# A planner's due times set anew, scores that wait for their evicted projections, and products of ones during the first loads

## The chip, the cores and the metric

The kernel runs on one core of one Trainium2 chip. The metric is the device time of one execution in microseconds (us). Each kernel is executed several times; the median and the spread are given, and one execution more is recorded by the hardware profiler. All arithmetic is in fp32.

The core's engines, as the profile names them: PE multiplies matrices (PEld is its loading of weights), DVE is the vector engine, ACT the scalar engine, POOL a second, slower vector engine, and SP issues DMA transfers. Each engine works off its own list of instructions in order. They wait for each other by semaphores. Products land in PSUM, in banks of 512 fp32 values for each of 128 partitions, and an engine has to evict them from there.

## The reference

Eight images of 64 x 64 pixels with 256 channels pass through two layers.

```python
# layer 0
q, k = split(x @ w_qkv + b_qkv);  v = k
ctx_h = sdpa(windows of 8 rows,    channels   0..127, 4 heads of 32)
ctx_v = sdpa(windows of 8 columns, channels 128..255, 4 heads of 32)
hv = hard_swish(v)
context = hard_swish(concat(ctx_h, ctx_v) + depthwise_conv3x3(hv) + dw_bias)
x = context @ w_out + b_out
# layer 1: attention over all 4096 pixels, with one head of 32
f, g, h = x @ kf + bf, x @ kg + bg, x @ kh + bh
beta = softmax(g @ f.T)
out = gamma * ((beta @ h) @ kv + bv) + x
```

kf, kg, kh and kv are the weights divided by their spectral norm, which the kernel works out at the start. sdpa is softmax attention, with a scale of 1/sqrt(32). A window has 512 pixels.

## The kernel before

**Units and steps.** The work of an image is cut into units: eight horizontal windows h0 to h7, eight vertical windows v0 to v7, and two halves l0 and l1 of the global attention, each with 2048 queries against all keys. A unit of h has 4 steps, one of v 3, one of l 32. All eight images run as one list of steps. The h0 of the next image is placed between v7 and l0 of this one, so that PE has scores to work on while f, g and h are being made.

A step does the same on PE everywhere: the products of the scores s (L849 and L825 in the windows, L1064 in l), from which ACT makes the weights p by two instructions of exp (L606), and then the products of the step before with the values, num (L878, L871, L1080). In v two of three steps have three passes instead of two (L825, with exps L838 and L843). The weights lie in a ring of eight slots. Before a slot is written again, DVE must have added up what it holds (L887, L895, L902; in l L1095) or a DMA issued by POOL must have (L1104, L1106), since the sums over the keys are needed for the softmax: DVE and DMA add steps together, and a product with ones on PE adds over the partitions (sum_h and sum_v L917, sum_l L1117). A v unit uses all eight slots.

**Fillers.** Between scores and values PE does everything else: the projections pq of an image (L326; tile m = 0 is q and m = 2 is k of the channels of h, called near; m = 1 and 3 are q and k of the channels of v, called far), the sums, the products pf (L987) and phd (L1014) that make f, g and h with w_out folded into their weights (wcomb), the transposes ph of h (L1028), and the results (w_out and the part of layer 1, evicted to ot_l at L1146). A projection has 16 products in four pieces. All fillers share one bank of PSUM, named mm, so one of them can only begin once the one before it has been evicted. The results take the banks of the scores instead. A result has two pieces, one for each 128 output channels, which take PE 8 us each.

**Around it.** x comes in tiles of 512 pixels (L663) into a pool of two buffers. Each q and k is evicted by ACT with its bias (qh L682, kh L697, qv L685). DVE transposes k (kt L766), and it goes through DRAM (kvia L771) and comes back as values (vs L782). The contexts of v go through DRAM as well (via_v L940, shuf_v L945). The convolution's nine taps for a pair of windows are one ACT instruction (L752) and eight on DVE (L756). f and g go through a tile fg and are spread by ten issues for each piece (L1004, L1005). All of these transfers, loads and stores alike, are issued on one queue, SP, strictly in order.

**The planner.** The order of instructions isn't written out. A class Flow plays the program forward at build time. It keeps a clock for each engine, advanced by constants (SCORES 0.96, VALUES 0.88, PROD 0.86, DRAIN 0.11 and so on, L71 to L77), and lanes of waiting tasks, each with a due step. The due steps come from the dictionary DUE (L49), as offsets from the first step of the unit that uses the task's outcome. `step` (L251) issues the scores, then urgent fillers, then the values, and then fills PE, ACT and DVE up to the clock. `require` issues whatever a step can't do without, no matter when it was due, and returns the time at which it ends. Before its scores a unit requires what stands in `u.ahead` (`unit_scores`, L1560): near q and near k for h, all far projections for v, and pf, ph and their transposes for l. The time that `require` returns for these is not used, so the planner's clock of PE goes on as if the scores could start at once. Near projections get their due steps at L1380 to L1386; for the first image first_near is added to both. The sum of an l unit is added at L1280, at a price of 1.5 products. Results wait in a lane of their own, and `apart` is the least number of steps between two pieces of them.

Of the kernel before, what the change touches and what calls it, by code (L numbers as in the profile page):

```python
# [17 lines left out]
P = 128  # L18
# [22 lines left out]
def side(h):  # L41
# [5 lines left out]
SLOTS = 8  # L47

DUE = dict(  # L49
    ahead1=104, ahead2=7, ahead3=1, ahead4=17, k0=-13, k1=52, k2=-18, k3=0, k4=-3, k5=18, k6=-3, k7=7,  # L50
    q0=70, q1=31, q2=-14, q3=-2, q4=70, q5=4, q6=0, q7=99, join_h0=38, join_h1=17, join_h2=23,
    join_h3=23, join_h4=-12, join_h5=26, join_h6=-17, join_h7=58, join_v0=26, join_v1=19, join_v2=20,
    join_v3=-25, join_v4=-148, join_v5=-22, join_v6=22, join_v7=-5, swish1=98, swish2=-48, swish3=-133,
    swish4=17, far_swish0=101, far_swish1=5, far_swish2=-23, far_swish3=28, far_swish4=46,
    far_swish5=-127, far_swish6=3, far_swish7=-2, result0=121, result1=-27, release_v=-9, norm_v=11,
    sums_v=-54, context_v=-34, clip_v=70, other=-91, first_ready=42, first_near=-1, first_k=1,
    first_q=-2, first_swish_v=-3, first_swish_h=54, first_conv_h=6, first_conv_v=22, near_k=-4,
    near_q=91, near_values=-10, clip=141, swish=12, conv_h0=168, conv_h1=16, conv_h2=24, conv_h3=39,
    conv_v0=17, conv_v1=23, conv_v2=29, conv_v3=69, tap=-21, join_h=-73, join_hl=24, join_v=1,
    context=-43, norm=18, release=-7, sums=66, add=26, adds_h=1, adds_v=0, group_h=0, group_v=1,  # L60
    add2=-44, add3=93, apart=6, fg0=-7, fg2=31, fg3=120, h0=32, h1=12, values_v=-74, near0=-55,
    spread0=4, spread1=72, spread_mid=61, conv_first=309, far_swish=-2,
)
INSIDE = 4
AHEAD = 16
# [4 lines left out]
SCORES, VALUES, PROD, TURN, DRAIN, PASS, THIRD = 0.96, 0.88, 0.86, 0.65, 0.11, 0.43, 0.5  # L70
EXP, EVICT, COPY, VIEW = 0.97, 0.62, 0.52, 0.42  # L71
# [26 lines left out]
class Flow:  # L98
# [5 lines left out]
    def __init__(self):  # L104
        self.t = 0
        self.clock = dict(pe=0.0, act=0.0, dve=0.0, sp=0.0)
        self.lanes = dict(pe=[], turn=[], act=[], dve=[], sp=[], pool=[], rows=[], res=[])
        self.open = None
        self.held, self.held_more, self.values_due = None, 0.0, False
        self.bank_free = 0.0  # L110
        self.half_end = self.exp_end = 0.0
        self.weights_free = self.mid_free = 0.0
        self.third = False
        self.apart = 0
        self.dve_last = None

    def add(self, lane, *args, **kw):
        task = Task(*args, **kw)
        task.lane = lane
        self.lanes[lane].append(task)  # L120
        return task
# [129 lines left out]
    def step(self, scores, values, passes=2, third=False):  # L251

        c = self.clock
        more = (passes - 2) * PASS
        rest = None
        self.third = passes > 2
        self.apart += 1
        self.values_due = True  # L260
        for task in self.waiting("res"):
            if self.apart >= DUE["apart"] and task.begin() <= c["pe"] + DRAIN or not scores:
                self.apart = 0
                c["pe"] = max(c["pe"] + DRAIN, self.half_end + LAG)
                while not task.done:
                    self.fill_act(c["pe"] + 4 * PROD)
                    self.run(task)
                    self.fill_dve()
        if scores:
            rest = scores()  # L270
            c["pe"] = max(c["pe"], self.banks()) + DRAIN + SCORES + more
            self.third = third
            self.half_end = max(c["act"], c["pe"] - more + PE_LAG, self.weights_free) + EXP
            if more:
                self.half_end = max(self.half_end, c["pe"] + PE_LAG) + EXP
            before, self.exp_end = self.exp_end, self.half_end + EXP
            c["act"] = self.exp_end
        else:
            before = self.exp_end
            c["pe"] = self.half_end = self.exp_end = max(c["pe"], c["act"], c["dve"]) + 3.0  # L280
        for task in sorted(self.waiting("turn"), key=lambda k: k.due):
            if self.begin(task) <= c["pe"] + 0.1:
                self.run(task)
        urgent = sorted((k for k in self.lanes["pe"] if k.due <= self.t), key=lambda k: k.due)
        if len(urgent) > 1 and urgent[0] in self.waiting("pe"):
            if self.begin(urgent[0]) <= c["pe"] + 0.1:
                self.require(urgent[0])
        if self.held:
            ready = self.held()
            c["pe"] = max(c["pe"] + DRAIN, before + LAG, ready + LAG) + VALUES + self.held_more  # L290
        self.held, self.held_more, self.values_due = values, more, False
        if rest:
            rest()
            if self.mid_free > self.exp_end - EXP:
                self.exp_end = c["act"] = self.mid_free + EXP
        self.fill_act(self.late(c["pe"]) - EVICT)
        self.fill_pe()
        self.fill_act(self.late(c["pe"]) + SLACK)
        self.fill_dve()
        for task in self.waiting("sp"):  # L300
            if task.begin() <= self.clock["pe"] + 0.5:
                self.run(task)

        for task in self.waiting("rows"):
            if task.begin() <= self.clock["pe"] + 0.5:
                self.run(task)
        for task in self.waiting("pool"):
            if task.begin() + BEHIND <= self.clock["pe"]:
                self.run(task)
        self.t += 1  # L310
# [19 lines left out]
def tile_attention_blocks(  # L330
# [18 lines left out]
    nc = tc.nc  # L349
# [14 lines left out]
    def mm_tile(name):  # L364
        return ps_mm.tile([P, TB], F32, tag="mm", name=name)
# [4 lines left out]
    ones = const.tile([P, P], F32, name="ones")  # L370
    nc.gpsimd.memset(ones, 1.0)
    three = const.tile([P, 1], F32, name="three")
    nc.gpsimd.memset(three, 3.0)
    three_e = const.tile([P, 1], F32, name="three_e")

    wqkv_sb = const.tile([P, 2, 2 * C], F32, name="wqkv_sb")
    wq = w_qkv.rearrange("(k p) m -> p k m", p=P)
# [142 lines left out]
    def attention(images, load_x, out_rows, exact):  # L520
# [17 lines left out]
        act = [state.tile([P, 2, 2 * TB], F32, name=f"act{i}") for i in range(NB // 2)]  # L538
# [656 lines left out]
        flow = Flow()  # L1195
# [56 lines left out]
        for u in units:  # L1252
            if not u.kind:
                continue
            e = u.t + u.steps
            w = [weights_ready(u.t + c) for c in range(u.steps)]
            if u.kind == "l":
# [12 lines left out]
                for c in range(0 if exact else u.steps):  # L1270
# [6 lines left out]
                    readers[u.t + c].append(task)  # L1277
                    gathered.append(task)
                total = flow.add(
                    "pe", [(u.sums, [("pe", PROD * (1 if exact else 1.5)), ("act", COPY)])], e + 1,  # L1280
                    [chain, *gathered[-2:]], ready=e, bank=True,
                )
                in_turn("sum", total)
# [1 line left out]
            else:  # L1285
# [12 lines left out]
                last = len(u.terms) - 1  # L1298
# [65 lines left out]
        for n, im in enumerate(ims):  # L1364
            last = ims[n - 1] if n else None
# [3 lines left out]
            for i in range(NB):  # L1369
                u = h[i]  # L1370
# [4 lines left out]
                start = last.l[0].t if last else 0  # L1375
# [4 lines left out]
                for m in (0, 2):  # L1380
                    near[i, m] = flow.add(
                        "pe", product_pieces(partial(im.project, i, m), 2, ("act", EVICT)),
                        (u.t + DUE["near_k" if m else "near_q"] + (0 if last else DUE["first_near"]))
                        if due is None else due, [], after, ready, True,
                    )
                early = start + inside_due(i, 0) if i in (1, 2) else u.t  # L1386
# [16 lines left out]
                for half in range(2):  # L1403
# [18 lines left out]
                    if p >= 0:  # L1422
# [3 lines left out]
                        if half and last and k == 0:  # L1426
                            due = min(due, start + inside_due(2 * HV[1], 0) + DUE["conv_first"])
                        tap = flow.add(
                            "act", [(partial(im.conv, p, half, (0,)), [("act", EXP)])],
                            due + DUE["tap"],  # L1430
                            scaled + [edges[q, half] for q in range(k, min(NB, k + 3)) if (q, half) in edges],
                            last.results[k] if last else [],
                        )
# [13 lines left out]
            context = {}  # L1447
# [74 lines left out]
        for n, im in enumerate(ims):  # L1522
            for i in range(INSIDE + 1 if n else 0, NB):
                more = [] if n else [im.far[i, 1], im.far[i, 3]]
# [31 lines left out]
        def left_by(kept):  # L1556

            return [k for n, mid in kept for k in ([last_mids[n]] if mid else readers[n])]

        def unit_scores(u, c):  # L1560
            if u.kind:
                flow.require(*u.ahead.get(c, ()))
                flow.weights_free = flow.require(*left_by(old[u.t + c][0]))
                if exact and c == 0 and flow.open:
                    flow.require(flow.open)
            rest = u.scores(c)
            if not rest:
                return None

            def then():  # L1570
                flow.mid_free = flow.require(*left_by(old[u.t + c][1]))
                rest()

            return then
# [8 lines left out]
        with tc.manual_schedule():  # L1583
            last = None
            steps = [(u, c) for u in units for c in range(u.steps)]
            passes = [3 if u.kind in ("h", "v") and c in u.passes else 2 for u, c in steps] + [2]
            for n, (u, c) in enumerate(steps):
                if c == 0 and n:
                    last = steps[n - 1][0]
# [31 lines left out]
        exact=False,  # L1621
# [4 lines left out]
    with tc.If(fine < 2 * P):  # L1626
        with tc.For_i(0, B) as b:
# [6 lines left out]
                exact=True,  # L1634
# [46 lines left out]
```

## Time and profile before

| | |
|---|---|
| time, median of 3 executions | 3267.01 us (3264.59 to 3268.1) |
| profiled execution, its own time | 3267.18 us |
| span of that execution in the trace | 3265.4 us |
| granted TensorE clock, mean | 0.999 |
| exps L606: busy, mean of one | 1612.8 us, 1024 ns |
| adds of l on DVE, L1095: busy, mean of one | 842.8 us, 1756 ns |
| convolution taps on DVE, L756: busy, mean of one | 654.0 us, 1278 ns |
| load of x (512 KB), issue to landing | 4.0 us |

The span begins with the first and ends with the last instruction, 1.8 us less than the time that is measured from outside. In the profile a line such as "s<-gq,f 32*128 32x512" reads: tile s is made from gq and f, with the partitions and elements of both operands. An arrow behind it names what the engine waited for. "Busy" of PE means that a product was in the array's pipeline. An image takes some 402 us. Image 4, which is looked at most, has its h7 at about 1760 us, its v0 to v7 from there to about 1865, and the l units behind that.

### The profile page before, as it was taken

Reading aid. Unit: us, or ns where it says so; the run is one execution under the profiler, and the core shown is the slowest. Engines: PE = TensorE matmul, PEld = TensorE weight load, DVE = VectorE, ACT = ScalarE, POOL = GpSimd, SP = SyncE. Lnnn points to the kernel's source line nnn. Section 1 sums busy time; section 2 is a strip of 40 time slices with the busy share of each in tenths; the row PEclk is TensorE's granted clock in tenths of the full one; section 3 lists DMA queues with packets and bytes.
Section 4 is the critical chain, followed back from the end, with each engine's and each line's share of the span. In section 5 each row is a group of like instructions: output and inputs, shape, how many; then the busy total and the mean of one; then the engine's idle time right before and its main releaser. Section 6 shows DMA issues by size and latency. Waiting matters only on the chain.

```text
span 3265.4 us, 83524 instructions
## 1 busy us (share of the span) xinstructions
PE 3218.2 (99%) x35348; PEld 1166.6 (36%) x35348; DVE 2659.7 (81%) x2426; ACT 2653.4 (81%) x3230; POOL 516.4 (16%) x786
## 2 busy tenths in 40 slices
PE   8999999999999999999999999999999999999998
PEld 3353233532335323343333433334323343234422
DVE  6898599975999669996699966998769986689865
ACT  6788788887888878888778887788877888778875
POOL 1002220022200222002210032100321003210132
PEclk9999999999999999999999999999999999999999
DMA  2235552356423564235642366423654236532465
GB/s 81 63 94 117 131 114 83 90 118 132 105 88 94 115 139 105 79 99 116 137 103 77 104 122 132 102 75 103 128 127 103 74 105 132 118 104 63 112 125 108
DMA packets 320655, 344.41 MB, mean 105 GB/s; under 512 B 33600, under 2 KB 198352, under 8 KB 320272
## 3 DMA queue, kind: packets, MB, share of 16 engines
q0 software_dynamic: 72000, 134.40, 23.2%
q1 hardware_dynamic: 246752, 204.04, 21.0%
q8 instruction: 280, 4.59, 0.6%
q14 instruction: 103, 0.84, 0.1%
q10 hardware_dynamic: 1520, 0.54, 0.1%
HBM read 99.78 MB, written 83.89 MB: 56 GB/s over the span
## 4 chain that ended last, share of the span: by engine, by line
PE 84%; DVE 9%; ACT 3%; DMA 2%; issue 1%; SPq 0%; DVEq 0%; ACTq 0%
PE s L1064 17%; PE num_l L1080 15%; PE pq L326 12%; PE s L849 8%; PE s L326 7%; PE num_h L878 6%; PE s L825 4%; PE num_v L871 4%; PE sum_v L917 3%; DVE act L756 3%; PE sum_h L917 3%; PE pf L987 1%; DVE acc_v L887 1%; PE num_v L878 1%; ACT p L606 1%
## 5 line engine op out<-in xcount | busy, mean ns | idle before, releaser
L606 ACT ACTIVATE p<-s 128x1024 f32<-128x1024 f32 x1664 | 1612.8, 1024 | 232.9 <-PE s L1064 143.8
L1095 DVE TENSOR_TENSOR acc_l<-acc_l,p 128x1536 f32<-128x1536 f32 x480 | 842.8, 1756 | 361.6 <-ACT p L606 357.4
L756 DVE SCALAR_TENSOR_TENSOR act<-hv,dw_sb,act 128x1024 f32<-128x1024 f32 x512 | 654.0, 1278 | 25.9 <-ACT act L752 16.5
L1064 PE MATMUL s<-gq,f 32*128 32x512 f32 x4096 | 594.1, 640 | 1.1 <-ACT ot_l L1146 1.1
L326 PE MATMUL pq<-x,wqkv_sb 128*32 128x256 f32 x8192 | 547.1, 381 | 14.0 <-DMA x<-in_xT 10.6
L1080 PE MATMUL num_l<-p,h_sb 128*32 128x512 f32 x4096 | 545.5, 605 | 0.3 <-ACT nums_l L1110 0.3
L326 PEld LDWEIGHTS pq<-x,wqkv_sb 128*32 128x32 f32 x8192 | 264.4, 110 | 431.8 <-issue 283.2
L849 PE MATMUL s<-qh,kh 32*128 32x512 f32 x2048 | 295.3, 640 | 14.0 <-ACT qh L682 13.9
L1106 POOL DMA_DIRECT2D acc_l<-p x240 | 210.3, 876 | 515.2 <-ACT p L606 477.7
L1106 POOL DMA_DIRECT2D row_l<-p x240 | 210.8, 878 | 426.9 <-ACT p L606 414.1
L878 PE MATMUL num_h<-p,vs 128*32 128x512 f32 x2048 | 272.0, 603 | 0.2 <-ACT nums_h L929 0.2
L1064 PEld LDWEIGHTS s<-gq,f 32*128 32x128 f32 x4096 | 168.7, 182 | 260.7 <-issue 247.1
L326 PE MATMUL s<-act,wout_sb 128*32 128x512 f32 x2048 | 229.2, 597 | 0.0
L1080 PEld LDWEIGHTS num_l<-p,h_sb 128*32 128x32 f32 x4096 | 80.7, 108 | 383.8 <-issue 371.3
L825 PE MATMUL s<-qv,kv 32*128 32x256 f32 x3072 | 214.3, 394 | 1.1 <-ACT p L843 0.8
L1146 ACT ACTIVATE ot_l<-s,bias_o 128x512 f32<-128x512 f32 x120 | 76.2, 684 | 161.3 <-PE s L326 154.5
L871 PE MATMUL num_v<-p,vs 128*32 128x256 f32 x3072 | 192.2, 383 | 0.0
L825 PEld LDWEIGHTS s<-qv,kv 32*128 32x128 f32 x3072 | 141.3, 183 | 80.5 <-issue 49.5
L1104 POOL DMA_DIRECT2D acc_l<-p x16 | 9.1, 566 | 1015.9 <-ACT sum_sb_h L626 508.8
L838 ACT ACTIVATE p<-s 128x1024 f32<-128x1024 f32 x128 | 131.8, 1030 | 33.5 <-PE s L825 33.4
L895 DVE TENSOR_TENSOR acc_h<-acc_h,p 128x2048 f32<-128x2048 f32 x64 | 146.1, 2282 | 7.8 <-ACT p L606 7.1
L887 DVE TENSOR_TENSOR acc_v<-p 128x2048 f32<-128x2048 f32 x64 | 146.3, 2286 | 6.4 <-PE sum_h L917 3.5
(153 smaller groups left out, 3211.5 us busy)
## 6 DMA issues: line engine op xcount, KB each, us to landing
acc_l<-p POOLq DMA_DIRECT2D x256, 256.0 KB, 3.3
row_l<-p POOLq DMA_DIRECT2D x256, 256.0 KB, 3.3
x<-in_xT SPq DMA_DIRECT2D x92, 512.0 KB, 4.0
kvia<-kt SPq DMA_DIRECT2D x128, 256.0 KB, 2.5
vs<-kvia SPq DMA_DIRECT2D x512, 64.0 KB, 2.1
out<-ot_l SPq DMA_DIRECT2D x120, 256.0 KB, 2.1
via_v<-nums_v SPq DMA_DIRECT2D x64, 256.0 KB, 2.1
shuf_v<-via_v SPq DMA_DIRECT2D x256, 64.0 KB, 2.1
```

The lines of the kernel that those rows point to most:

```text
L326: nc.tensor.matmul(out[quad(r), :], lhsT=lhsT[:, quad(r)], rhs=rhs, start=start, stop=stop)
L606: nc.scalar.activation(pt[:, 2 * z : 2 * z + 2, :], sc[z], AF.Exp, scale=scale)
L756: nc.vector.scalar_tensor_tensor(o, src, wt, o, ALU.mult, ALU.add)
L825: mm = nc.tensor.matmul(place_of(n, r, h, sc), lhsT=k[quad(r), t * P : (t + 1) * P], rhs=q[quad(r), side(h)], start=True, stop=True,)
L849: nc.tensor.matmul(row_of(sc, r), lhsT=k[quad(r), c * P : (c + 1) * P], rhs=q[quad(r), :], start=True, stop=not exact,)
L871: nc.tensor.matmul(u["num"][quad(r), side(h)], lhsT=vs[kind, i][:, r, t, :], rhs=place_of(n, r, h, (pt[:, :2], u["mid", c], pt[:, 2:])), s ...
L878: nc.tensor.matmul(u["num"][quad(r), :], lhsT=vs[kind, i][:, r, c, :], rhs=u[c][:, r, :], start=(c == 0), stop=(c == 3),)
L917: nc.tensor.matmul(u["sum"][quad(r), cols], lhsT=ones[:, :D], rhs=pt, start=(n == 0), stop=(n == last),)
L1064: nc.tensor.matmul(row_of(sc, r), lhsT=f4[quad(r), c * P : (c + 1) * P], rhs=gq[quad(r), z, :], start=True, stop=not exact,)
L1080: nc.tensor.matmul(u["num"][quad(r), :], lhsT=h_sb[:, c, :], rhs=u[c][:, r, :], start=(c == 0), stop=(c == 4 * NB - 1),)
L1095: nc.vector.tensor_add(acc, u[0][:, :rows, :] if c == 1 else acc, u[c][:, :rows, :])
L1106: nc.gpsimd.dma_start(out=u["row", c % 2], in_=u[c][:, rows, :], accum_op=ALU.add)
```

## The change

It has five parts. All values of DUE are set anew, and one key is new (first_near_q). `unit_scores` keeps the time at which the required tasks end, and `step` starts PE's clock for the scores no earlier than that. The sums of l are priced at two products instead of 1.5. Nine products of a 128 x 128 tile of ones with itself are issued ahead of the first loads, into the bank of the fillers; nothing reads what they leave. And in the first image the due step of near q comes from first_near_q alone, and that of near k from first_near alone, rather than near_q + first_near and near_k + first_near.

Of the values of DUE the ones that are spoken of below: apart from 6 to 1, near_q from 91 to 100, near_k from -4 to -7, near0 from -55 to -163, sums_v from -54 to 5, fg2 from 31 to 12, fg3 from 120 to 64, result0 from 121 to 320, result1 from -27 to -118.

```diff
 DUE = dict(
-    ahead1=104, ahead2=7, ahead3=1, ahead4=17, k0=-13, k1=52, k2=-18, k3=0, k4=-3, k5=18, k6=-3, k7=7,
...
-    add2=-44, add3=93, apart=6, fg0=-7, fg2=31, fg3=120, h0=32, h1=12, values_v=-74, near0=-55,
-    spread0=4, spread1=72, spread_mid=61, conv_first=309, far_swish=-2,
+    first_near_q=-1, ahead1=164, ahead2=14, ahead3=2, ahead4=57, k0=-11, k1=25, k2=-19, k3=1, k4=0,
...
+    adds_h=1, adds_v=0, group_h=0, group_v=1, add2=-19, add3=231, apart=1, fg0=-8, fg2=12, fg3=64, h0=2,
+    h1=13, values_v=-91, near0=-163, spread0=2, spread1=57, spread_mid=60, conv_first=264, far_swish=22,
 )
@@ class Flow: __init__
+        self.scores_ready = 0.0
@@ step
             rest = scores()
-            c["pe"] = max(c["pe"], self.banks()) + DRAIN + SCORES + more
+            c["pe"] = max(c["pe"] + DRAIN, self.banks() + DRAIN, self.scores_ready) + SCORES + more
@@ tile_attention_blocks
+    warm = mm_tile("warm")
+    for _ in range(9):
+        nc.tensor.matmul(warm[:, :P], lhsT=ones, rhs=ones, start=True, stop=True)
+
     wqkv_sb = const.tile([P, 2, 2 * C], F32, name="wqkv_sb")
@@ attention
-                    "pe", [(u.sums, [("pe", PROD * (1 if exact else 1.5)), ("act", COPY)])], e + 1,
+                    "pe", [(u.sums, [("pe", PROD * (1 if exact else 2)), ("act", COPY)])], e + 1,
...
-                        (u.t + DUE["near_k" if m else "near_q"] + (0 if last else DUE["first_near"]))
+                        u.t + (DUE["near_k" if m else "near_q"] if last else DUE["first_near" if m else "first_near_q"])
                         if due is None else due, [], after, ready, True,
@@ unit_scores
-                flow.require(*u.ahead.get(c, ()))
+                flow.scores_ready = flow.require(*u.ahead.get(c, ()))
```

More of the change, by code (lines that the diff above doesn't have):

```diff
@@ L49 @@
 DUE = dict(
-    ahead1=104, ahead2=7, ahead3=1, ahead4=17, k0=-13, k1=52, k2=-18, k3=0, k4=-3, k5=18, k6=-3, k7=7,
[L51 to L60, printed above, removed]
@@ L61 @@
-    add2=-44, add3=93, apart=6, fg0=-7, fg2=31, fg3=120, h0=32, h1=12, values_v=-74, near0=-55,
-    spread0=4, spread1=72, spread_mid=61, conv_first=309, far_swish=-2,
+    first_near_q=-1, ahead1=164, ahead2=14, ahead3=2, ahead4=57, k0=-11, k1=25, k2=-19, k3=1, k4=0,
+    k5=68, k6=8, k7=94, q0=35, q1=-22, q2=89, q3=-17, q4=47, q5=-5, q6=5, q7=59, join_h0=71,
+    join_h1=-163, join_h2=21, join_h3=-424, join_h4=6, join_h5=13, join_h6=-157, join_h7=62, join_v0=35,
+    join_v1=18, join_v2=-2, join_v3=-34, join_v4=-158, join_v5=-181, join_v6=-28, join_v7=-208,
@@ new lines @@
+    swish1=67, swish2=-47, swish3=-101, swish4=-67, far_swish0=282, far_swish1=-127, far_swish2=125,
+    far_swish3=-80, far_swish4=36, far_swish5=-43, far_swish6=-107, far_swish7=6, result0=320,
+    result1=-118, release_v=-60, norm_v=10, sums_v=5, context_v=-71, clip_v=167, other=-52,
+    first_ready=110, first_near=-7, first_k=1, first_q=-3, first_swish_v=-49, first_swish_h=-51,
+    first_conv_h=6, first_conv_v=43, near_k=-7, near_q=100, near_values=-42, clip=161, swish=88,
+    conv_h0=133, conv_h1=25, conv_h2=30, conv_h3=43, conv_v0=26, conv_v1=21, conv_v2=96, conv_v3=76,
@@ L63 @@
+    tap=-26, join_h=-28, join_hl=48, join_v=-5, context=-37, norm=9, release=-92, sums=167, add=-87,
+    adds_h=1, adds_v=0, group_h=0, group_v=1, add2=-19, add3=231, apart=1, fg0=-8, fg2=12, fg3=64, h0=2,
+    h1=13, values_v=-91, near0=-163, spread0=2, spread1=57, spread_mid=60, conv_first=264, far_swish=22,
 )
```

## The prediction

> **What bounds the kernel now.** I read busy shares first, then PE's waits, then the start and one image in the timeline, last the stretches of 20 us.
>
> ```profile
> PE 3218.2 (99%) x35348; PEld 1166.6 (36%) x35348; DVE 2659.7 (81%) x2426; ACT 2653.4 (81%) x3230; POOL 516.4 (16%) x786
> ```
>
> PE is busy 3218.2 of 3265.4 us. Only about 47 us are open to a change that leaves the products as they are. A busy PE is not PE at its peak, so I also took, from the trace, the distance from start to start of equal products: scores 1.07 us, values 0.88, a sixteen-instruction piece of a projection 0.98, one of 32 1.84. Where the distance exceeds that, PE was held up. The waits of PE name who held it (total, times, longest):
>
> ```profile
> PE s L849 <- ACT qh L682: 13.9, 14, 1.2
> PE pq L326 <- DMA x<-in_xT: 10.6, 7, 5.6
> ...
> PE sum_l L1117 <- DMA row_l<-p: 2.3, 4, 1.1
> ...
> PE ph L1028 <- ACT h L1022: 0.8, 1, 0.8
> ...
> PE sum_h L917 <- DVE acc_h L895: 0.8, 1, 0.8
> ```
>
> The first two rows are half of what there is. Here is one place of both, h7 of image 4 (columns: start, length, engine, line, operation; in brackets the idle time and its releaser):
>
> ```profile
> 1757.99 0.61 PE L326 MATMUL pq<-x,wqkv_sb 128*32 128x256 f32 x8
> ...
> 1759.10 0.69 ACT L682 ACTIVATE qh<-pq,bqkv_sb 128x512 f32<-128x512 f32 x1
> 1759.84 1.14 PE L849 MATMUL s<-qh,kh 32*128 32x512 f32 x8 [1.23 <-ACT qh L682]
> ...
> 1763.15 1.93 PE L326 MATMUL pq<-x,wqkv_sb 128*32 128x256 f32 x32 [1.17 <-DMA x<-in_xT]
> ```
>
> The q projection is issued directly ahead of the scores that need it. PE waits for the eviction to qh; 3 us later it waits again, for the x tile of the next image.
>
> **Scores wait for evicted projections; due steps anew.** This makes no instruction faster. It moves instructions, so I compared the issue order of both kernels, engine by engine.
>
> *q of h7.* In images 1 to 6 the scores after the last piece start 1.30 us late by start-to-start distance, six times. In the changed order about 8.7 us of other PE work lie between that projection and the scores in images 1, 3, 4 and 6; in 2 and 5 it still stands directly ahead. An eviction takes 0.69 us, so it is hidden there: 4 x 1.30 = **-5.2 us**. In image 0 all eight q projections still stand directly ahead of their scores, despite the new due time: 8 x 0.88 us stay.
>
> *x for the next image.* Before, this load is queued on SP behind kvia and the four vs loads of h7, which wait for DVE's transpose. In the changed order it stands right after the kvia load before those, some 9 us earlier, and its buffer is free by then: 9.3 us of PE work or more lie between release and use, where a load needs 4.0 to land (page, DMA issues). What it is moved past, kvia and vs, is not delayed much: one issue of 0.4 us. The row has 10.6, of which 5.6 is the start of the kernel; the remaining six waits are 5.0 us, by start-to-start 6.1. I take **-5.5**.
>
> *sum of h7, image 0.* It moves behind the values of v0, so its wait for acc_h goes: **-0.9**.
>
> *sums of l.* The factor 1.5 to 2 changes only the planner's clock; the instructions stay. The row (2.3 us, four times) is bounded by 0 and -2.3, or as much again if the new due step brings it nearer its DMA. I take 0.
>
> *Results of l closer together* (apart 6 to 1): both pieces of 8.07 us now come one step apart instead of some five. They use the banks of the scores and are emptied by ACT. The nearest row is the scores after such a piece, 1.1 us for two waits, 0.55 each. With 15 pairs this is bounded by 0 and +8; a step's scores and values lie between the two, so I take 0.
>
> *f and g of the last image.* Here the order turns against the change:
>
> ```profile
> 3053.41 1.93 PE L987 MATMUL pf<-act,wcomb 128*32 128x256 f32 x32
> ...
> 3067.07 0.66 PE L1028 MATMUL ph<-ident,h 128*128 128x128 f32 x4 [0.81 <-ACT h L1022]
> 3067.65 1.14 PE L1064 MATMUL s<-gq,f 32*128 32x512 f32 x8
> ```
>
> From that pf to the first scores of l0 run the eviction, ten SP issues of about 0.6 us (the last gq issue at 3064.78) and a landing of 2 us: 12.1 us, which PE's work just covered. Counted by durations, PE's work between the two was 11.2 us and becomes 8.5, since pf comes a step later: **+2.8**, once. In images 0 to 6 there are 21.5 us of work, so nothing. The transposes of h come sooner after their projection; the wait (0.8 once) could come again, but two images had this spacing before without it: 0.
>
> **DVE.** Its work in l1, h and v is regrouped, without change in amount: two taps of the convolution move from l1 towards h and v, sums and joins move by some units. Two stretches of image 4 (length, busy PE, PEld, DVE, ACT, POOL, clock, DMA share, GB/s):
>
> ```profile
> 1800.00:1820.00 20.00, 20.00 (x284) 10.18 (x280) 19.51 (x22) 18.19 (x22) 0.00 (x0) 1.00 0.36 105
> ...
> 1860.00:1880.00 20.00, 20.00 (x240) 7.72 (x236) 13.10 (x16) 16.98 (x24) 0.00 (x0) 1.00 0.36 100
> ```
>
> In v DVE has 2 to 5% of slack; behind it, it has plenty. Adding DVE's durations up to the same add in both orders, the changed kernel is 7 us ahead at the end of l1, about even at v0 to v3, 3.2 to 3.9 us behind at v5, and even again at v7. Behind that add stand exps on ACT, which need the slot of the weights that it reads, and behind these scores and values on PE. In the trace ACT's exps once wait 1.73 us for such an add,
>
> ```profile
> 1850.48 1.94 ACT L606 ACTIVATE p<-s 128x1024 f32<-128x1024 f32 x2 [1.73 <-DVE acc_v L887]
> ```
>
> and PE in that stretch loses 0.2 us. So about 1.5 us of lateness is covered; the rest (up to 2.4) is lost unless the planner moved the sum of v5 late enough, which it did by one step (about 3 us). Bounds: 0 to 8 x 2.4 = +19. Nearest row: 0.2 for each of eight images, taken as **+2**.
>
> **Ones times ones.** The start:
>
> ```profile
> 0.89 0.20 POOL L371 MEMSET ones<- 128x128 f32 x1
> ...
> 5.61 3.64 PE L326 MATMUL pq<-x,wqkv_sb 128*32 128x256 f32 x32 [5.61 <-DMA x<-in_xT]
> ...
> 10.05 3.64 PE L326 MATMUL pq<-x,wqkv_sb 128*32 128x256 f32 x32 [0.80 <-ACT kh L697]
> ```
>
> Both first projections take 3.64 us; at 1763.15 the same takes 1.93. The granted clock of this stretch reads 1.00, so the row of the clock doesn't show it, the durations do: 2 x 1.71 = 3.4 us are lost. The nine products: a projection is 32 instructions of 256 columns, four side by side, in 1.93 us, so 0.24 us in a row, 0.12 for 128 columns; each fp32 product is two instructions, so 18 x 0.12 = 2.2 us, and 4.1 at the start's pace (x 3.64/1.93). From 1.2 they end by about 5.3, ahead of x at 5.61: they cost nothing. If they ended later by 1 us they would cost 1.
>
> What do they bring? By the row, products were still slow 8 us after the first, with a gap of 0.8 us between, and quick by 15.57; so from 1.2 on the change of pace would come after 9.3: only the second projection gains, -1.7. [...] I take the row, **-1.7**, with 0 and -3.4 as ends.
>
> **Sum.** -5.2 - 5.5 - 0.9 + 2.8 + 2 - 1.7 = -8.5 us. From the profiled execution's 3267.18 this gives 3258.7; the median of the runs lies 0.2 below, so 3258.5. With the ends above (stalls removed fully, warm -3.4, DVE 0: -13; warm 0, half of the x loads still late, +4 from DVE: -2) this case ranges from 3253 to 3265.
>
> **Rivals.** *DVE in v4 to v6 becomes the bound.* For it: 95 to 98% busy there, and 3.2 to 3.9 us more ahead of v5's add. Against: 1.73 us of lateness cost PE 0.2, and the planner knows DVE's clock. Price: the whole 3.5 in each of eight images is +28; with 1.5 covered +16. Without the +2 of the sum the change stands at -10.5, so +5.5 to +17.5: 3273 to 3285, middle 3279. It decides from 1.3 us for each image on.
>
> *The waits return elsewhere.* The x load moved earlier meets another one, or the earlier projection holds the single bank that fillers share, so that another eviction is waited for. For it: that bank already has rows, such as pq after qv in image 0. Against: uses of the bank closer than 1.9 us are about as many as before. Then half of the 10.7 us from q and x is left: -3, 3264.
>
> *It doesn't do what it says.* The products of ones don't raise the pace, and the new rule has no hold on q: in image 0 the order shows that it has none. Without -1.7, and with two of the four h7 still late (+2.6): -4.2, 3263.
>
> **How the numbers follow.** Chances: forecast 0.58, DVE 0.18, return 0.16, no hold 0.08. This kernel's measurement tells about 0.2% (6.5 us) from no change: faster means under 3260.5. Of the forecast some 0.5 lie there, of the others 0.05: 0.55; within 0.2%: 0.27; slower: 0.18, nearly all DVE's. The range is the forecast's, down to 3250, and up to the DVE case's lower half, 3276.
>
> **What would show it.** Right: PE's wait for qh falls from 13.9 to about 9 us, that for x to about 5.6; the first two projections sum to 5.6 us rather than 7.3; one new wait of about 2.8 us for gq or f ahead of l0 in the last image. Wrong: exps that wait for acc_v in v5 by more than 1.5 us in every image, with PE waits for p behind them; waits on ot_l after the paired results; x waits in l that were not there.

## The result, and the profile after

The changed kernel takes 3254.59 us (median; 3253.14 to 3257.8, 7 runs), the one before 3267.01 us in the same session (also 7 runs): 12.4 us less, a ratio of 0.9965 with an interval of 0.9954 to 0.9977. Run again later, beside other kernels, it had 0.9973 (0.9962 to 0.9983). So it is faster, and by more than the 8.5 us that were forecast. The span of its profiled execution is 3252.7 us, 12.7 less than before.

The busy shares of the changed kernel:

```profile
PE 3220.7 (99%) x35366; PEld 1175.8 (36%) x35366; DVE 2660.4 (82%) x2426; ACT 2654.2 (82%) x3230; POOL 521.8 (16%) x786
```

DVE and ACT have the same work as before. PE is busy 2.5 us longer (the products of ones alone are 4.2), and its idle time fell from 47 to 32 us. The waits of PE say where (total, times, longest):

```profile
PE s L854 <- ACT qh L687: 8.9, 10, 1.2
...
PE phd L1019 <- ACT sum_sb_v L631: 1.4, 1, 1.4
PE s L830 <- ACT p L611: 1.3, 2, 1.1
...
PE sum_l L1122 <- DMA row_l<-p: 0.7, 2, 0.5
PE num_l L1085 <- ACT nums_v L934: 0.6, 1, 0.6
...
PE pq L327 <- DMA x<-in_xT: 0.3, 1, 0.3
```

Line numbers are up to five higher than before. What changed, row by row:

| | before | after | difference, us |
|---|---|---|---|
| first scores start at (timeline) | 14.50 | 11.42 | -3.1 |
| scores wait for qh | 13.9 | 8.9 | -5.0 |
| projections wait for x, without the kernel's first | 5.0 | 0 | -5.0 |
| sum_l waits for row_l | 2.3 | 0.7 | -1.6 |
| sum_h waits for acc_h | 0.8 | 0 | -0.8 |
| scores wait for ot_l | 1.1 | 0 | -1.1 |
| phd waits for sum_sb_v (last image) | 0 | 1.4 | +1.4 |
| v scores wait for p, L606 before, L611 after (image 0) | 0.2 | 1.3 | +1.1 |
| values wait for vs (image 0) and nums_v (last image) | 0 | 1.6 | +1.6 |
| sum | | | -12.5 |

The sum is within 0.2 us of the difference of the spans. What the table leaves out nearly cancels: smaller rows come to -1.1 (qv -1.4, wcomb +0.4 and some tenths), and apart from the start PE is busy 1.4 us longer. The start, in the timeline of the changed kernel:

```profile
1.15 4.21 PE L379 MATMUL warm<-ones 128*128 128x128 f32 x18 [1.15 <-POOL ones L372]
...
5.62 2.25 PE L327 MATMUL pq<-x,wqkv_sb 128*32 128x256 f32 x32 [0.27 <-DMA x<-in_xT]
...
8.68 1.93 PE L327 MATMUL pq<-x,wqkv_sb 128*32 128x256 f32 x32 [0.81 <-ACT kh L702]
```

The products of ones end at 5.36, just ahead of the first x tile. The first projection takes 2.25 us where it took 3.64, the second 1.93 where it took 3.64. Not all of the 3.1 us stays: behind this start the first values wait 0.46 us for vs (PE num_h, at 15.95), which they did not before. In the table that wait is part of the row of vs.

### The profile page after: what moved, and what is told of

Same layout as the page of the kernel before. It is cut to its first block, busy times and chain, and to the rows that moved or that the text cites. A ratio compares the mean times of both kernels' runs of the same rounds, so it can differ in the third digit from the quotient of the medians.

```text
span 3252.7 us, 83570 instructions
## 1 busy us (share of the span) xinstructions
PE 3220.7 (99%) x35366; PEld 1175.8 (36%) x35366; DVE 2660.4 (82%) x2426; ACT 2654.2 (82%) x3230; POOL 521.8 (16%) x786
## 4 chain that ended last, share of the span: by engine, by line
PE 94%; DVE 2%; ACT 2%; DMA 1%; issue 1%; SPq 0%; ACTq 0%; DVEq 0%; POOLq 0%
PE s L1069 17%; PE num_l L1085 15%; PE pq L327 12%; PE s L854 10%; PE num_h L883 7%; PE s L327 7%; PE s L830 6%; PE num_v L876 5%; PE sum_v L922 4%; PE sum_h L922 3%; PE num_v L883 2%; PE pf L992 2%; PE s L1141 1%; PE phd L1019 1%; PE sum_l L1122 1%
## 5 line engine op out<-in xcount | busy, mean ns | idle before, releaser
L611 ACT ACTIVATE p<-s 128x1024 f32<-128x1024 f32 x1664 | 1613.5, 1024 | 219.7 <-PE s L1069 130.0
L327 PE MATMUL pq<-x,wqkv_sb 128*32 128x256 f32 x8192 | 538.5, 380 | 2.5 <-ACT kh L702 0.8
L1111 POOL DMA_DIRECT2D acc_l<-p x240 | 210.4, 877 | 474.5 <-ACT p L611 423.5
L740 POOL MEMSET hv<- 128x18 f32 x64 | 16.2, 253 | 998.0 <-PE s L830 652.1
L892 DVE TENSOR_TENSOR acc_h<-p 128x2048 f32<-128x2048 f32 x64 | 146.0, 2282 | 5.4 <-PE sum_h L922 4.2
```

What stands on the lines that cost most here:

```text
L327: nc.tensor.matmul(out[quad(r), :], lhsT=lhsT[:, quad(r)], rhs=rhs, start=start, stop=stop)
L611: nc.scalar.activation(pt[:, 2 * z : 2 * z + 2, :], sc[z], AF.Exp, scale=scale)
L892: nc.vector.tensor_add(u["acc"], u["acc"] if c == 2 else u[0], u[c])
L1111: nc.gpsimd.dma_start(out=u["row", c % 2], in_=u[c][:, rows, :], accum_op=ALU.add)
```

## The experiments

Each kernel was timed against the kernel before, on the same chip as its neighbours in the same group. Where the changed kernel is the yardstick, its ratio in the second group, 0.9973, is the nearest; between groups about 0.001 (3 us) can't be told apart.

### The products of ones alone

Once they were taken out of the changed kernel, once added to the kernel before. The order of everything else stays.

```diff
-    warm = mm_tile("warm")
-    for _ in range(9):
-        nc.tensor.matmul(warm[:, :P], lhsT=ones, rhs=ones, start=True, stop=True)
```

> The changed kernel without the nine products of ones; every other instruction stands in the same order. Theory (the products only raise the pace of the first two projections, 7.28 us together before and 4.18 after): 3.1 us slower than the changed kernel, so about 9.3 us faster than the kernel before, ratio 0.9972; the two projections take 3.64 us each again. Rival (the start is covered by something else later): as fast as the changed kernel, ratio 0.9962.

> The kernel before plus the nine products of ones alone, order otherwise the same. Theory: 3.1 us faster than before, ratio 0.9990, with the qh waits (13.9 us) and the x waits (10.6 us, less the first) as they were. Rival (the gain at the start is given back at the next wait): ratio 1.0000.

Without them the changed kernel had 3258.44 us, ratio 0.9980 (0.9974 to 0.9987). With them the kernel before had 3261.59 us, ratio 0.9989 (0.9981 to 0.9997), 3 to 4 us faster. Both go the way of the theory, but the first is within what can't be told apart between groups (0.9980 against 0.9973); the second rests on its interval. There, too, the rival was partly right: of the 3.0 us that the first scores came earlier, 0.83 went into a wait of the first values for vs. The profile of the changed kernel without the products of ones has an odd start:

```profile
5.79 3.50 PE L327 MATMUL pq<-x,wqkv_sb 128*32 128x256 f32 x32 [5.79 <-DMA x<-in_xT]
10.10 1.93 PE L327 MATMUL pq<-x,wqkv_sb 128*32 128x256 f32 x32 [0.81 <-ACT kh L698]
```

Only the first projection is slow here; in the kernel before both were. So the same start costs 1.6 us in one execution and 3.4 in another, and what the products of ones are worth differs with it: by these profiles 1.4 us (first scores at 12.84 against 11.42) to 3.1.

The traces also keep the granted clock's own changes. Full clock begins at 14.31 us in the kernel before and at 6.32 in the changed kernel. The durations of the first two projections go with it. Without the products of ones they were 3.64 us each in the kernel before and in the one with its x load on POOL, 3.50 and 1.93 in the changed kernel without these products, 3.44 and 1.93 in the kernel before with the rule alone. With them the first took 1.93 to 2.43 us in four profiles (the changed kernel and its repeat, the kernel before with them, the changed kernel without the rule), and the second 1.93. That they bring the full pace forward is thereby shown.

### The rule alone, and the due steps alone

The rule that the scores' clock waits for the evicted projections was taken out of the changed kernel, and put alone into the kernel before:

```diff
-            c["pe"] = max(c["pe"] + DRAIN, self.banks() + DRAIN, self.scores_ready) + SCORES + more
+            c["pe"] = max(c["pe"], self.banks()) + DRAIN + SCORES + more
```

> The changed kernel with the new due steps, but without the rule that the clock of PE waits for the evicted projections. Theory (the due steps alone carry the gain: in this order q of h7 stands in the same places in images 1 to 6, and the x load too; the order differs in image 0, in the first step of some images and little else): within 1 us of the changed kernel, ratio 0.9962. Rival (the rule carries it): the 10 us of the waits for qh and x come back, ratio 0.999.

> The kernel before with the rule alone, old due steps. Theory: the sum of h7 in image 0 moves (-0.9 us), q of h7 stays directly ahead of its scores in images 1 to 6 and x_b_0 stays behind kvia and vs, so ratio 0.9997. Rival (the rule carries the gain): ratio 0.997.

Both expectations failed. New due steps without the rule: 3269.61 us, ratio 1.0018 (1.0011 to 1.0024), some 15 us slower than with it. The rule with the old due steps: 3269.75 us, ratio 1.0017 (1.0010 to 1.0023), slower than without it. The rule alone is no gain, and the change without the rule isn't either; only both together are.

What I had said of images 1 to 6 is true all the same. In the profile without the rule the waits for qh are 8.9 us, as in the changed kernel, and those for x are gone but for the kernel's first tile. Most of the loss, 10 us, lies in image 0; the rest comes in steps of about 1 us in images 2, 5, 6 and 7 and was not followed up. The timeline of image 0 between h7 and v0, where v0's first values need the last far projection to go through ACT, DVE, DRAM and back:

```profile
159.50 0.68 ACT L706 ACTIVATE kv<-pq,bqkv_sb 128x512 f32<-128x512 f32 x1
...
161.02 1.30 DVE L771 STREAM_TRANSPOSE kt<-kv 128x512 f32<-128x512 f32 x2
...
161.75 3.53 SPq L776 DMA_DIRECT2D kvia<-kt  x3
...
165.93 1.88 SPq L787 DMA_DIRECT2D vs<-kvia  x4
...
171.39 1.94 PE L883 MATMUL num_v<-p,vs 128*32 128x512 f32 x8 [7.24 <-DMA vs<-kvia]
```

From the eviction's start to the values 11.9 us pass. In the changed kernel the same eviction (kv) starts 4.6 us earlier, and PE then has two projections of the next image to do; it waits 0.5 us for vs:

```profile
154.89 0.68 ACT L706 ACTIVATE kv<-pq,bqkv_sb 128x512 f32<-128x512 f32 x1
...
163.75 1.06 PE L883 MATMUL num_v<-p,vs 128*32 128x512 f32 x8 [0.48 <-DMA vs<-kvia]
```

Without the rule those two projections stand ahead of the last far one, so it comes late and nothing is left to cover its way. Without the rule the planner's clock doesn't count image 0's eight waits for q, 0.88 us each; that this is why it chose another order there is argued, not shown. And the wait costs more than itself. The stretches around it (length, busy PE, PEld, DVE, ACT, POOL, granted clock, DMA share, GB/s):

```profile
164.00:172.00 8.00, 0.76 (x8) 0.23 (x8) 7.48 (x10) 3.78 (x4) 0.00 (x0) 0.78 0.79 212
172.00:176.00 4.00, 4.00 (x40) 2.02 (x36) 4.00 (x4) 0.62 (x1) 0.00 (x0) 0.59 0.02 7
176.00:180.00 4.00, 4.00 (x60) 1.94 (x56) 3.86 (x4) 3.90 (x5) 0.00 (x0) 1.00 0.02 4
```

Behind the wait, PE's clock is granted at 0.59 for some 4 us, and the values that end the wait take 1.94 us where the same take 1.06 in the changed kernel. By the first scores of image 0's l1 this kernel is 10 us behind the changed one, of 14.2 at its end.

The rule with the old due steps also loses in image 0, some 4 us there: exps wait 2.76 us for an add of v's sums at 174, PE waits 1.5 for them, and between 176 and 184 us its clock is granted at 0.51 and 0.64.

### The last far projection first

If order in image 0 was all, holding back the next image's projections should do the same as the rule. This kernel has the new due steps, not the rule, and this edit:

```diff
-                ready = start if inside else last.v[0].t + DUE["near0"] if last else ...
+                ready = start if inside else last.v[0].t + (DUE["near0"] if n > 1 else 0) if last else ...
```

> The kernel with the new due steps and without the rule, but with the near projections of image 1's h0 held back to the first step of v0, so that the last far projection of image 0 goes ahead of them again. Theory (the rule's whole worth is that order in image 0; without it v0 waited 7.2 us for its values and PE ran at half pace behind that wait): the wait falls to under 2.5 us, the slow stretch goes, ratio about 0.998. Rival (the rule is worth something in every image): ratio stays at 1.0018.

Failed: 3287.39 us, ratio 1.0071 (1.0057 to 1.0085). The far projection did go first (kv is evicted at 155.28). But of the two others only k still stood between it and the values; q came behind them, at 175.52, and v0's first scores had moved ahead of the eviction. That is a scores, a values and a projection less, some 3.8 us of PE's work. The way of the values was longer, too, 12.8 us rather than 8.9, as DVE began the transpose 2.6 us behind the eviction's start and not 0.8. Together that is about the wait of PE for vs, 8.4 us where the changed kernel has 0.5. In image 1 PE waited 4.1 us twice for nums_h behind projections that had been pushed on.

```profile
168.10 1.94 PE L883 MATMUL num_v<-p,vs 128*32 128x512 f32 x8 [8.40 <-DMA vs<-kvia]
```

So putting the far projection first isn't enough: by these traces it takes work of PE behind it as cover for the 9 to 13 us that its values need, and a DVE that is free for the transpose. No kernel was run that changes this one order and nothing else. In the same group the changed kernel stood as yardstick:

> The changed kernel once more, on the same chip as the three below, as their yardstick: ratio 0.9965 within its interval. Its distance to the kernel without the products of ones (ratio 0.9980 on another chip) is to be 1 to 4 us, as the first two projections run at the slow pace or not.

It had 3254.92 us, ratio 0.9973 (0.9962 to 0.9983). Its profile starts with a first projection of 2.43 us and a second of 1.93.

### q of h7

First with one value for all late windows, then with image 0 as well:

```diff
-    near_q=100
+    near_q=-1
```

> The changed kernel with one value edited: near_q from 100 to -1, so that q of h5 to h7 is due one step ahead. In this order q of h7 stands 10 us of PE work ahead of its scores in all of images 1 to 6, that is in images 2 and 5 too. Theory: two waits of 1.30 us go, 2.6 us faster than the changed kernel, ratio 0.9957. Rival (the projection, moved, takes the place of another filler that is then late): no gain, or x waits come back.

> As the one before, and first_near_q from -1 to -4, for the eight windows of image 0. In this order q of h1 to h3 stands 0.9, 4.3 and 0.9 us ahead of its scores, h0 and h4 to h7 as before; but k of h6 and h7 now stands directly ahead of q, so q waits for the bank. Theory: -2.6, -2.6 for three waits of 0.88, +1.6 for two bank waits of 0.8: 3.6 us faster than the changed kernel, ratio 0.9954. Rival (image 0 is held up elsewhere, by far projections or values): no better than with near_q alone.

The waits for q went as expected: PE's waits for qh fell from 8.9 to 6.5 and 4.2 us. Yet the kernels are slower than the changed one, 3269.3 us (ratio 1.0014, 1.0007 to 1.0021) and 3278.18 us (1.0041, 1.0027 to 1.0055). With near_q alone the profile shows two places. In v of images 2 and 5, exps wait up to 3.3 us for DVE's adds and PE up to 0.9 for the exps. From v3 on each of these images loses 5.6 us, of which 2.9 are waits of PE; the rest is not accounted for. And in the last image f and g are late, as the prediction had feared for the change itself:

```profile
3060.38 1.13 PE L1069 MATMUL s<-gq,f 32*128 32x512 f32 x4
3063.46 1.12 PE L1069 MATMUL s<-gq,f 32*128 32x512 f32 x2 [1.95 <-DMA gq<-fg]
3066.59 2.07 PE L1069 MATMUL s<-gq,f 32*128 32x512 f32 x2 [2.02 <-DMA gq<-fg]
```

with these stretches behind them:

```profile
3060.00:3065.00 5.00, 2.63 (x10) 0.81 (x8) 2.76 (x3) 1.61 (x2) 0.00 (x0) 1.00 0.45 107
3065.00:3070.00 5.00, 3.40 (x18) 1.21 (x22) 0.08 (x1) 1.02 (x1) 0.00 (x0) 0.51 0.32 82
3070.00:3075.00 5.00, 5.00 (x60) 1.84 (x56) 1.01 (x2) 1.20 (x3) 0.46 (x1) 0.81 0.00 0
```

Two waits of 2.0 us, and then the clock at 0.51: the first two instructions behind the second wait take 2.07 us where they took 1.12. Between the first scores of l0 and of l1 of this image the kernel falls back by a further 8.5 us against the changed one, for waits of 4.0. With first_near_q added, v0 of image 0 waits 5.9 us for vs again.

Then the same for h7 of images 2 and 5 alone, where the changed kernel still waits:

```diff
-  u.t + (DUE["near_k" if m else "near_q"] if last else ...)
+  u.t + ((DUE["near_k"] if m else -1 if i == NB - 1 and n in (2, 5) else DUE["near_q"]) if last else ...)
```

> The changed kernel with q of h7 due one step ahead in images 2 and 5 alone. In this order images 2 and 5 become the same as images 1, 3 and 4 from h6 to l0, but for one sum of h5 and one piece's split, and nothing else moves. Theory (near_q in all windows was slower because it moved DVE's work in v and the f and g of the last image, not because of q itself): the two waits of 1.30 us go and nothing comes, 2.6 us faster than the changed kernel, ratio about 0.9960 where the changed kernel has 0.9967. Rival (q ahead always costs as much elsewhere): same as the changed kernel or slower.

3249.88 us (3249.18 to 3251.48), ratio 0.9949 (0.9936 to 0.9963): the fastest kernel of this study. PE's waits for qh are down to image 0's eight:

```profile
PE s L854 <- ACT qh L687: 6.5, 8, 0.8
```

Unit by unit against the changed kernel's profile, image 2 gains 1.4 us between its h5 and h0 of the next, and image 5 gains 1.5. The whole span is 3.0 us shorter (3249.7 against 3252.7). The distance between the two medians, 4.7 to 5 us, is more than the 2.6 expected, and by the ratios it is 5 to 8 us, but they were taken in different groups. So it was not q ahead of its time that made near_q slow, it was all that moved with it.

### The x load's place in the queue

The kernel before, with the next image's second load of its first tile on POOL's queue:

```diff
-                nc.sync.dma_start(out=xt[i], in_=load_x(b, i))
+                (nc.gpsimd if again else nc.sync).dma_start(out=xt[i], in_=load_x(b, i))
```

Here again is true for the load of tile 0 of an image other than the first, if it was loaded once already.

> The kernel before, with the second load of the next image's first x tile issued by POOL instead of SP, so that it doesn't stand behind kvia and vs. PE's order is the same. Theory (the x waits come from the place in SP's queue): PE's waits for x in images 1 to 6, 5.0 us, go, ratio 0.9985. Rival (the tile is late for its buffer or its landing): they stay, ratio 1.0000.

3259.44 us, ratio 0.9981 (0.9972 to 0.9990), 6.5 us faster. The wait that is left is the kernel's first:

```profile
PE pq L326 <- DMA x<-in_xT: 5.9, 1, 5.9
```

That settles this part: the tile was late because of where its load stood on SP. Moving it is worth some 6 us: 6.5 by the medians (3 to 9 by the interval), 5.0 by the waits.

### How much cover v5 has

Needless reductions on DVE ahead of v5's first add, two and five of them; they took 0.68 us each. (Reductions and not adds, since the on-chip memory has no room for the 2 KB per partition that an add would write: with them, 0.0625 KB was left for another buffer of 2 KB.)

```diff
                 def add(c):
+                    if kind and i == 5 and not exact:
+                        for _ in range(2):
+                            nc.vector.tensor_reduce(idle, kv[:, i, :], AX.X, ALU.max)
```

> The changed kernel with two needless reductions of 512 columns on DVE (some 0.6 us each, 1.2 together) ahead of the first add of v5, in all eight images. Theory (v5's add is covered by 1 to 2 us): 0 to 1 us for each image, so 0 to 8 us slower than the changed kernel; exps wait for acc_v longer. Rival (DVE isn't near the path in v): no difference.

> The same with five reductions (some 3 us). Theory: 1 to 2 us for each image, 8 to 16 us slower than the changed kernel, with PE waiting for p in v5 or v6 in each image. Rival: under 3 us.

With two: 3263.21 us, ratio 0.9995 (0.9987 to 1.0004), some 8 us slower than the changed kernel. With five: 3287.52 us, ratio 1.0080 (1.0063 to 1.0097), 33 to 35 us slower, more than twice what was expected. In v5 of image 4 the exps wait 0.40 us for the add without the reductions (profile of the repeat) and PE not at all; 1.70 with two, and PE 0.45 and 0.20; with five:

```profile
1845.98 1.94 ACT L612 ACTIVATE p<-s 128x1024 f32<-128x1024 f32 x2 [3.86 <-DVE acc_v L896]
...
1847.06 2.99 PE L831 MATMUL s<-qv,kv 32*128 32x256 f32 x20 [2.61 <-ACT p L612]
```

The difference between the wait of the exps and that of PE is the cover: 3.86 - 2.61 = 1.25 us, and 1.70 - 0.65 = 1.05. And here too the clock falls:

```profile
1844.00:1848.00 4.00, 1.39 (x12) 0.59 (x12) 4.00 (x4) 2.02 (x3) 0.00 (x0) 0.79 0.45 110
1848.00:1852.00 4.00, 4.00 (x28) 1.83 (x28) 3.86 (x6) 3.26 (x5) 0.00 (x0) 0.50 0.31 102
1852.00:1856.00 4.00, 4.00 (x53) 1.72 (x48) 3.59 (x5) 2.08 (x4) 0.34 (x3) 0.85 0.23 66
```

A wait of 2.61 us in image 4 puts the kernel 5.8 us further back by the first scores of image 5's h0: 2.6 for the wait, about as much for the pace. In image 2, and again in image 5, a pf waits 2.15 us for a context from DVE, behind the reductions. There the clock stays (1.00 in image 2), and the kernel falls back by 2.7 us:

```profile
1048.34 1.27 PE L996 MATMUL pf<-act,wcomb 128*32 128x256 f32 x18 [2.15 <-DVE act L976]
```

```profile
1048.00:1052.00 4.00, 3.66 (x60) 2.26 (x64) 4.00 (x6) 2.98 (x4) 0.00 (x0) 1.00 0.46 108
```

## Why the prediction was right, and where not

**The sum.** The rows that were to bring time, q, x and the sum of h7, brought 10.8 us of 11.6. The other differences are sizes: the products of ones brought 1.4 more, and two rows taken as 0 brought 2.7. The two losses, +4.8 together, came as +4.1, but for the most part as other waits in other places (the last three rows of the table); that their size agrees is luck. The range's lower end should have been 3254 by its own sum, not 3253.

**q of h7, -5.2: right.** The waits for qh fell by 5.0, in images 1, 3, 4 and 6, while 2 and 5 kept theirs, and image 0 its eight. The last experiment on q shows that the other two could go as well.

**x for the next image, -5.5: right.** Measured -5.0, and moving the load to another queue in the kernel before brought it by itself (6.5).

**Sum of h7 in image 0, -0.9: right** (0.8 in the waits).

**Ones times ones, -1.7: right in kind, too small in this execution.** The first scores came 3.1 us earlier. I took the row (slow products 8 us after the first), by which only the second projection gains; both gained, and the end of -3.4, all that the start lost, was nearer. The step that failed is the time of the change of pace, which the row put at 9.3 us: full clock began at 6.32, 5.2 us after the first product of ones, so the first projection lost only 0.3 us (2.25 against 1.93). Nor is the loss the same in every profile: kernels without the products of ones had one slow projection in two of them (3.50 and 3.44 us) and two in two others (3.64 each). An expected value between 1.5 and 3 would have been better than either.

**Sums of l and scores behind results, both taken as 0: mis-sized.** They gave -1.6 and -1.1. For the sums the profiles decide: their waits for row_l are 1.8 to 2.6 us in the four kernels with the old due steps, and 0.7 at most in the ten with the new ones. So the change brought it, and without the rule there are none either. Whether the new due steps did it or the price of two products, which all ten have as well, was not tested. The waits for ot_l come and go between executions of the same order: without the products of ones they were 1.2 us where the changed kernel had none. That part is not shown to come from the change.

**f and g of the last image, +2.8: half right.** The last image did lose: of 16.3 us that the changed kernel was ahead at h7 of image 7, 12.5 are left at its l1. But not for the reason given. In the changed kernel's timeline

```profile
3050.16 0.59 SPq L1010 DMA_DIRECT2D gq<-fg  x1
...
3051.27 1.93 PE L1019 MATMUL phd<-act,wcomb 128*32 128x256 f32 x32 [1.42 <-ACT sum_sb_v L631]
...
3054.60 1.14 PE L1069 MATMUL s<-gq,f 32*128 32x512 f32 x8
```

gq is issued at 3050.16 and lands at 3052.15, before the scores at 3054.60 want it. PE had waited before: phd needs the fillers' bank, which was still to be emptied of a sum, and that had to wait on ACT. Two other waits, 0.6 for nums_v and 0.5 for nums_h, lie there too. With near_q moved, the wait for gq did appear, twice 2.0 us; the mechanism is real. What was mis-sized here is the chain: 12.1 us from pf's end to the landing were taken over from the kernel before, and 8.4 were measured. In the kernel before, the eviction to fg began 1.2 us behind pf's end, behind exps that had waited for DVE, and the first issue on SP another 1.5 us behind it; in the changed kernel both follow within 0.1 us.

```profile
3054.72 1.94 ACT L606 ACTIVATE p<-s 128x1024 f32<-128x1024 f32 x2 [1.51 <-DVE acc_v L887]
3056.54 0.69 ACT L996 ACTIVATE fg<-pf,bcomb 128x512 f32<-128x512 f32 x1
```

```profile
3043.81 0.69 ACT L1001 ACTIVATE fg<-pf,bcomb 128x512 f32<-128x512 f32 x1 [0.67 <-PE pf L992]
...
3044.52 2.42 SPq L1009 DMA_DIRECT2D f<-fg  x4
```

**DVE in v, +2: no loss there in images 1 to 6.** The one new wait for p, 1.1 us, is in image 0. v5's add, 3.2 to 3.9 us later by the count of durations, kept exps waiting for 0.4 us at most in the profile of the repeat, since its sum on PE had been moved as well; at v6 they waited for up to 1.97 us, at no cost to PE. The figure for the cover, 1.5 us, was near: 1.05 to 1.25. The rival that DVE decides was wrong for this change but described its neighbours well: 1.4 us more of DVE's work at v5 is 8 us, 3.4 us more is 33 to 35.

**What failed is what the prediction didn't price: the rule.** It said that the change "moves instructions", compared the two orders as a whole, and took image 0 as unchanged except for one sum. In the rival it even held that the rule "has no hold on q". It has none, as the order said. But without it the changed kernel is 15 us slower, 10 of them in image 0, and with the old due steps it costs 5. The total came out right since the order compared was that of both together. A sentence such as "the due steps bring this, the rule that" can't be made from it.

**The price of a wait.** The forecast counted each wait with its own length. For the waits for q and x, of 1.0 to 1.3 us, that held: they came and went one for one. For waits above 2 us it held where the clock stayed (2.15 cost 2.7) and not where it fell (2.6 cost 5.8). The rival's upper price, 28 us for 3.5 us in eight images, was therefore low: 3.4 us cost 33 to 35.

## What to carry to other kernels

A planner's constants and its rules are tuned as one: test a rule with the due times that it was tuned with, and don't credit either with the gain. When an instruction is moved, look for what it had covered, for the nearest chain through DRAM and for the queue that its loads stand in. If one wait is to be removed, move that one instruction in those stages alone; the broad setting that does the same everywhere moves others too.

## What the runs showed of the hardware

A wait of PE of some 2 us can cost twice its length in this kernel, since the granted clock fell to about half behind several of them: 0.59 after a wait of 7.2 us, 0.51 after two of 2.0, 0.50 after one of 2.6, 0.51 after 1.5 and other short ones within 10 us. It is not certain: the wait of 2.15 us in image 2 above left the clock at 1.00. Short waits vary as well. In the changed kernel one of 1.1 us at 174 us left the clock alone:

```profile
176.00:180.00 4.00, 4.00 (x58) 1.92 (x59) 3.96 (x5) 3.29 (x4) 0.00 (x0) 1.00 0.22 66
```

In the same order without the products of ones a wait of 1.0 us at the same place was followed by

```profile
176.00:180.00 4.00, 4.00 (x26) 1.16 (x28) 3.96 (x5) 2.86 (x4) 0.00 (x0) 0.57 0.24 70
```

26 instructions on PE for 58, at a clock of 0.57. What decides between the two is not shown.

How long such a fall lasts can be read in the changed kernel: the clock is at 0.50 from 129.20 to 132.61 us, for 3.41 us; a wait of PE of 1.20 us for woutT_sb had ended 1.4 us before. As an estimate from these numbers, that costs half of 3.41, 1.7 us. In v5 of image 4 with five reductions the clock stands at 0.79, 0.50 and 0.85 for 4 us each: by the same estimate 3.4 us are lost there, and with the wait of 2.61 that makes 6.0, where 5.8 were measured.

Last, the granted clock in the profile reads 1.00 in the first 14 us of the kernel before, where products run at about half pace (3.64 us for the 1.93 of later). The trace has no entry for the clock before 14.31 us, and the view takes the missing as full.
